# A planner's durations, and where third products stand, in a two-layer graph kernel on one core

## The chip, the core and the metric

The kernel runs on one core of one Trainium2 chip. The metric is the device time of one execution in microseconds (us), the median of several runs. Five engines work side by side and meet at semaphores: PE (TensorE, matrix products), DVE (VectorE), ACT (ScalarE), POOL (GpSimd) and SP (SyncE, which here only issues transfers).

## The reference, cut to what matters

`x` has the shape 64 x 256 x 512, `adj` is a 256 x 256 matrix of zeros and ones, about 3% of them ones. Two layers follow each other, each with a layer norm and a ReLU ahead of it and a residual around it.

```python
h = jnp.maximum(_layernorm(x, axis=-1), 0.0)
q, k, v = h @ Wq.T, h @ Wk.T, h @ Wv.T
rel = adj.T[None] * jnp.einsum('bnd,bmd->bnm', q, k)
rel = rel / jnp.linalg.norm(rel, axis=2, keepdims=True)
x = x + jnp.einsum('bnm,bmd->bnd', rel, v)
h = jnp.maximum(_layernorm(x, axis=-1), 0.0)
y = jnp.einsum('nm,bmd->bnd', adj, h)
x = x + jnp.einsum('bnd,do->bno', y, weight) + bias
```

## The kernel before, in words

**Work in pairs.** Two of the 64 batches are worked on at once, as a pair of 512 rows: 32 pairs. `Wq` and `Wk` are multiplied into one matrix m ahead of everything, so that scores are h m h'.

**Three products for one.** Every operand of a product with full precision is kept as three parts: u (the value rounded by a scaled copy on ACT), l (what is left) and s (a cross term of both). A bank of PSUM gets the u products, then the l products; ACT then scales the bank in place by a number close to one (line 361); then the third products, those of s, are added. So third products wait for a scaling, and the scaling waits for the l products. The parts are made by `split_right_ps` (ACT makes u at line 265, DVE s at line 266, DVE l from s at line 268) and by `split_left_ps` (ACT u at 274, DVE l at 275, DVE s at 276).

**Stages of a pair**, by operand names in the profile: `g_stage` (h with m, four banks, split into gy_u, gy_l, gy_s), `v_stage` (h with wv, four blocks, split into `v_low` and `late_parts`), `scores` (h with gy, two banks of 256-column products; then multiplied by adj into `h_rel`, squared and summed), `gather` of the pair before (adj with the second layer's h), `turn_scores` (scores turned and split into rel_u, rel_l and rel_s), `mix` of the pair before (gy, now holding y, with w), `attend` (rel with v, four banks). Scores are turned by 16 small transfers and DVE (lines 480 to 487) or, in pairs 0, 1 and 31, by PE (line 467).

**Who decides the order.** The kernel doesn't emit its instructions one after another. Stages call `plan.add(engine, cost, fn, reads, writes)`, and `Plan.order` (lines 58 to 102) then lays down one order for all engines. Costs and landing times are in microseconds. The matmul groups keep the order in which they were added. From their running sum each op gets a due time, going back over what depends on it. A list scheduler then runs through model time: on the engine that comes free first, it takes, of the ops that are ready at that moment, the one that is due first. It never keeps an engine idle for an op that becomes ready a little later. Between engines it counts `SYNC`, 0.12. On the chip every engine works through its own list in order.

**`unit`** (lines 349 to 367) is one bank. `first` yields the u and l products (three groups in `three`, lines 369 to 388: two of u, one of l; two groups in `attend`, u and l). Then `finish` runs what waits in the list `waiting`, which is the third products of the bank before and its drain. Then it adds the scaling and puts its own third products into `waiting`:

```python
        for cost, fn, reads in first(ps):
            plan.add("PE", cost, fn, reads, [key])
        finish(plan)
        ...
        plan.add("ACT", 0.49, lambda: A.activation(ps, ps, AF.Copy, scale=ONE), [], [key])
```

So the third products of one bank stand behind both the u and the l products of the next. Ahead of `scores` stands v block 1 (right operand wv_s). Ahead of `attend` stands the last bank of `mix` (w_s); in pair 31 it is v block 3, and in pair 0 nothing, as line 725 calls `finish` first.

Of the kernel before, what the change touches and what calls it, by code (L numbers as in the profile page):

```python
# [27 lines left out]
class Plan:  # L28


    SYNC = 0.12
# [26 lines left out]
    def order(self):  # L58
        ops = self.ops
        at, ideal = 0.0, {}  # L60
        for n, (engine, cost, *_) in enumerate(ops):
            if engine == "PE":
                ideal[n] = at
                at += cost
        due = [ideal.get(n, at + 50.0) for n in range(len(ops))]
        for n in range(len(ops) - 1, -1, -1):
            engine, cost, _, before, _, early = ops[n]
            due[n] -= early
            for m in before:
# [44 lines left out]
def kernel(  # L114
# [142 lines left out]
    MM, HALF = 0.231, 0.1185  # L257
# [3 lines left out]
    def split_right_ps(plan, ps, key, parts, names, at, cost=0.49):  # L261
# [4 lines left out]
        plan.add("DVE", 0.63, lambda: V.scalar_tensor_tensor(  # L266
            s(), f(u()), ONE, ps, op0=ALU.mult, op1=ALU.subtract), [*key, *ku], ks)
        plan.add("DVE", 0.6, lambda: V.scalar_tensor_tensor(  # L268
            l(), f(s()), -CROSS, f(u()), op0=ALU.mult, op1=ALU.add), [*ku, *ks], kl)

    def split_left_ps(plan, ps, key, parts, names, at):
        u, l, s = (p(at) for p in parts)
        ku, kl, ks = names
        plan.add("ACT", 0.49, lambda: A.activation(u, ps, AF.Copy, scale=NEAR), [key], ku)
        plan.add("DVE", 0.6, lambda: V.tensor_sub(l, ps, f(u)), [key, *ku], kl)  # L275
        plan.add("DVE", 0.6, lambda: V.scalar_tensor_tensor(
            s, f(l), CROSS + 1.0, ps, op0=ALU.mult, op1=ALU.subtract), [key, *kl], ks)
# [3 lines left out]
    def load(plan, i, src=None, name="fresh"):  # L281

        dst = fresh if name == "fresh" else ring[i % 2]
        plan.add("SP", 0.65, lambda: SP.dma_start(out=dst, in_=xs[i]), [], keys(name, TC), lands=5.5)

    def norm(plan, i, layer, src, name):

        st, mv, rs, nb = stats[layer][i % 2]
        k = f"n{layer}{i % 2}"
        for c in range(TC):  # L290
            def chunk(c=c):
                V.bn_stats(st[:, c, :], src[:, c, :])  # L292
                V.bn_aggr(mv[:, c, :], st[:, c, :])
            plan.add("DVE", 0.84, chunk, [(name, c)], [(k, c)])
        every = keys(k, TC)
        plan.add("DVE", 0.12, lambda: V.tensor_scalar(
            rs, mv[:, :, 1], 0.0, EPS, op0=ALU.max, op1=ALU.add), every, [(k, "rs")])
# [5 lines left out]
        plan.add("DVE", 0.25, end, every, [(k, "rs")])  # L303

        def relu(dst, c):
            A.activation(dst, src[:, c, :], AF.Relu, bias=nb[:, c : c + 1], scale=rs[:, c : c + 1])
        return relu, [(k, "rs")]

    def h_rows(plan, i, src=fresh, name="fresh"):
        relu, needs = norm(plan, i, 0, src, name)  # L310
        for c in range(TC):
            plan.add("ACT", 0.72, lambda c=c: relu(h_rel[:, c, :] if name == "x0" else h_cols[:, c], c),
                     [(name, c), *needs, *([("h_rel", 0)] if c else [])], [("h_rel", c)] if c else keys("h_rel", TC))
# [4 lines left out]
    def h_turn(plan):  # L318
        def turn(k):
            ht[k] = room(f"ht{k}", 2, T, tag=f"h_s{k}")  # L320
            for d in range(2):
                V.transpose(ht[k][:, d].rearrange("p (c k s) -> p c k s", c=TC, k=J), h_placed[:, :, 2 * k + d])  # L322
        for k in range(2):
            plan.add("DVE", 1.16, lambda k=k: turn(k), placed_all, [("h_s", 2 * k), ("h_s", 2 * k + 1)])
# [6 lines left out]
    def h_parts(plan):  # L331
        u, l = h
        for k in range(2):
# [5 lines left out]
            plan.add("DVE", 1.14, lambda k=k, at=at: V.tensor_sub(  # L339
                l[:, at], ht[k], f(u[:, at])), [*ks, *ku], kl)  # L340
            plan.add("DVE", 1.14, lambda k=k: h_third(k), [*ku, *kl], ks)
# [7 lines left out]
    def unit(plan, first, second, drain, on=None):  # L349
# [3 lines left out]
        if on is not None:  # L353
            plan.add("ACT", 0.58, lambda: A.copy(ps, on), ["bias"], [key])
        for cost, fn, reads in first(ps):
# [5 lines left out]
        plan.add("ACT", 0.49, lambda: A.activation(ps, ps, AF.Copy, scale=ONE), [], [key])  # L361
# [67 lines left out]
    def scores(plan, i):  # L429
        rn = norms[i % 2]  # L430
        for b in range(NB):
# [7 lines left out]
            def drain(ps, key, b=b):  # L439
# [4 lines left out]
                plan.add("DVE", 0.6, lambda: V.tensor_mul(  # L444
# [3 lines left out]
                for k in range(NC):  # L448
                    plan.add("ACT", 0.53, lambda k=k: A.activation(
                        columns(ps)[:, k], dst[:, k], AF.Square, accum_out=rn[:, b, k : k + 1]),  # L450
                        [("h_rel", b)], [key, (f"rn{i % 2}", b, k)])
            unit(plan, first, second, drain)

    def turn_scores(plan, i):
# [3 lines left out]
        plan.add("DVE", 0.12, lambda: V.reciprocal(rn, rn), [], sums)  # L458
        if by_pe(i):
            u, l = (part.rearrange("p b t k n -> p b (t k n)") for part in rel_p)  # L460
            for b in range(NB):
# [11 lines left out]
                plan.add("ACT", 0.49, lambda ps=ps, b=b: A.activation(  # L473
                    u[:, b], ps, AF.Copy, scale=NEAR), [key], [("rel_u", b)])
                plan.add("DVE", 0.63, lambda ps=ps, b=b: V.tensor_sub(  # L475
                    l[:, b], ps, f(u[:, b])), [key, ("rel_u", b)], [("rel_l", b)])
                plan.add("DVE", 0.6, third, [("rel_u", b), ("rel_l", b)],
# [4 lines left out]
        for b in range(NB):  # L482
            for k in range(NC):
                plan.add("DVE", 0.33, lambda b=b, k=k: V.transpose(
# [11 lines left out]
        plan.add("DVE", 1.14, lambda: V.tensor_sub(l, flat_raw(), f(u)), [*halves, *rel_u], rel_l)  # L496
        plan.add("DVE", 1.14, lambda: V.scalar_tensor_tensor(
            whole(rel_third()), f(l), CROSS, f(u), op0=ALU.mult, op1=ALU.subtract), [*rel_u, *rel_l], halves)

    def attend(plan, i, exact):  # L500
        slot, rn = i % 2, norms[i % 2]
        for c in range(TC):
# [16 lines left out]
            def drain(ps, key, b=b, n=n, c=c):  # L519
                plan.add("DVE", 0.63, lambda: V.scalar_tensor_tensor(  # L520
# [4 lines left out]
            unit(plan, first, second, drain)  # L525

    def layer_1(plan, i, exact):
        slot = i % 2
        relu, needs = norm(plan, i, 1, ring[slot], f"x{slot}")
        for c in range(TC):  # L530
            x_c = [(f"x{slot}", c), *needs]
            if not exact:
                plan.add("ACT", 0.72, lambda c=c: relu(changing("late", "h2", 8, D)[:, c], c), x_c,
# [4 lines left out]
            plan.add("ACT", 0.72, lambda c=c: relu(raw()[:, c % 2], c), x_c,  # L538
                     [("raw", 0), ("raw", 1)] if not c else k)
            plan.add("ACT", 0.53, lambda c=c, u=u: A.copy(late(u), raw()[:, c % 2]), k, [("late", u)])  # L540
            plan.add("DVE", 0.6, lambda c=c, u=u, l=l: V.tensor_sub(
# [29 lines left out]
    def mix(plan, i, blocks_of=range(4)):  # L571
        slot = i % 2
        for c in blocks_of:
# [5 lines left out]
            def drain(ps, key, c=c):  # L579
                plan.add("DVE", 0.6, lambda: V.tensor_add(  # L580
# [64 lines left out]
    adjt = []  # L645
# [4 lines left out]
    def first_turn(plan):  # L650

        u, l = h
        for d in range(DC):
# [6 lines left out]
            plan.add("ACT", 0.49, lambda ps=ps, d=d: A.activation(  # L660
                u[:, d], ps, AF.Copy, scale=NEAR), [key], [("h_u", d)])
            plan.add("DVE", 0.63, lambda ps=ps, d=d: V.tensor_sub(
                l[:, d], ps, f(u[:, d])), [key, ("h_u", d)], [("h_l", d)])
        for k in range(2):
            kept = [(f"h_{q}", d) for q in "ul" for d in (2 * k, 2 * k + 1)]
            plan.add("DVE", 1.14, lambda k=k: h_third(k), kept, [("h_s", 2 * k), ("h_s", 2 * k + 1)])
# [7 lines left out]
    def first_g(plan):  # L674

        banks = [next_bank() for _ in range(DC)]
        for k in range(3):
            for e, (ps, key) in enumerate(banks):
# [3 lines left out]
                if k == 2:  # L682
                    plan.add("ACT", 0.49, lambda ps=ps: A.activation(ps, ps, AF.Copy, scale=ONE), [], [key])
# [21 lines left out]
    def pairs(exact):  # L705
# [6 lines left out]
        plan.add("ACT", 0.49, lambda: A.copy(adjt[0].rearrange("p m n -> p (m n)"), bank[6]), [("bank", 6)], ["adjt"])  # L712
# [83 lines left out]
```

## Time and profile before

| | us |
|---|---|
| median of 3 runs | 1561.76 (1561.21 to 1562.63) |
| the profiled execution | 1560.76 |
| its span, first to last instruction | 1559.0 |

The profile is of one execution. Its span is 1.76 us shorter than the time of that same execution. In three stretches the engines were busy as follows (us; the answer to a question for stretches of the span):

| stretch | length | PE | DVE | ACT |
|---|---|---|---|---|
| 24.7 to 66 | 41.30 | 39.33 | 40.93 | 28.13 |
| 800 to 847.4 (one pair) | 47.40 | 47.40 | 41.82 | 31.89 |
| 1511 to 1530 | 19.00 | 18.24 | 17.43 | 12.31 |

"Busy" on PE is to be read with care, since a matmul's end is modelled and not measured. The distance from one matmul's start to the next is the better measure. "Late start" below means: later than the regular distance of that shape.

### The profile page before, as it was taken

Reading aid. Unit: us, or ns where it says so; the run is one execution under the profiler, and the core shown is the slowest. Engines: PE = TensorE matmul, PEld = TensorE weight load, DVE = VectorE, ACT = ScalarE, POOL = GpSimd, SP = SyncE. Lnnn points to the kernel's source line nnn. Section 1 sums busy time; section 2 is a strip of 40 time slices with the busy share of each in tenths; the row PEclk is TensorE's granted clock in tenths of the full one; section 3 lists DMA queues with packets and bytes.
Section 4 is the critical chain, followed back from the end, with each engine's and each line's share of the span. In section 5 each row is a group of like instructions: output and inputs, shape, how many; then the busy total and the mean of one; then the engine's idle time right before and its main releaser. Section 6 shows DMA issues by size and latency. Waiting matters only on the chain.

```text
span 1559.0 us, 22543 instructions
## 1 busy us (share of the span) xinstructions
PE 1548.2 (99%) x8046; PEld 1323.5 (85%) x8046; DVE 1355.3 (87%) x2419; ACT 1022.7 (66%) x1941; POOL 24.3 (2%) x39
## 2 busy tenths in 40 slices
PE   9999999999999999999999999999999999999998
PEld 6788888888888888888888888888888888888886
DVE  6997889898889988898988899888989888989786
ACT  5567666666667676666676675766666766666654
POOL 0000000000000000000000000000000000000000
PEclk9999999999999999999999999999999999999999
DMA  5321333223333223333233332233332233322211
GB/s 199 112 83 41 122 111 120 77 71 110 118 113 119 66 78 117 114 117 90 72 96 118 112 122 68 77 114 114 116 106 71 81 121 111 120 71 76 85 55 56
DMA packets 91112, 153.63 MB, mean 99 GB/s; under 512 B 17136, under 2 KB 32240, under 8 KB 90992
## 3 DMA queue, kind: packets, MB, share of 16 engines
q1 hardware_dynamic: 80768, 116.46, 24.7%
q0 software_dynamic: 8432, 32.51, 5.7%
q10 hardware_dynamic: 1792, 3.15, 0.6%
q8 instruction: 65, 1.06, 0.3%
q14 instruction: 55, 0.45, 0.1%
HBM read 70.78 MB, written 33.55 MB: 67 GB/s over the span
## 4 chain that ended last, share of the span: by engine, by line
PE 95%; DVE 3%; DMA 1%; ACT 0%; issue 0%; ACTq 0%; DVEq 0%
PE bank L255 95%; DMA bias_bc<-in_L_gnn_bias_dram 1%; DMA x_ring<-in_x_dram 1%; DVE late_parts L266 0%; DVE late_parts L268 0%; DVE rel_s_parts L470 0%; DVE st L292 0%; DVE rel_l L475 0%; DVE gy_l L275 0%; DVE m_l L268 0%; DVE gy_l L268 0%; DVE wv_l L268 0%; DVE ht L322 0%; DVE wv_s L266 0%; DVE m_s L266 0%
## 5 line engine op out<-in xcount | busy, mean ns | idle before, releaser
L361 ACT ACTIVATE bank<-bank 128x512 f32<-128x512 f32 x572 | 333.5, 583 | 307.8 <-PE bank L255 304.2
L255 PE MATMUL bank<-wv_s,hs 128*128 128x512 f32 x512 | 137.8, 391 | 0.0
L255 PE MATMUL bank<-wv_u,h_u 128*128 128x512 f32 x512 | 137.5, 390 | 0.0
L255 PE MATMUL bank<-wv_l,h_l 128*128 128x512 f32 x512 | 136.9, 389 | 0.0
L255 PE MATMUL bank<-w_u,gy_u 128*128 128x512 f32 x512 | 136.9, 389 | 0.0
L255 PE MATMUL bank<-w_l,gy_l 128*128 128x512 f32 x512 | 136.9, 389 | 0.0
L255 PE MATMUL bank<-h_l,m_l 128*128 128x512 f32 x512 | 136.6, 389 | 0.1
L255 PE MATMUL bank<-w_s,gy_s 128*128 128x512 f32 x512 | 136.7, 389 | 0.0
L255 PE MATMUL bank<-h_u,m_u 128*128 128x512 f32 x512 | 136.5, 389 | 0.0
L255 PE MATMUL bank<-hs,m_s 128*128 128x512 f32 x512 | 136.4, 389 | 0.0
L266 DVE SCALAR_TENSOR_TENSOR gy_s<-gy_u,bank 128x512 fp32r<-128x512 f32 x128 | 86.2, 675 | 43.0 <-ACT gy_u L265 43.0
L255 PEld LDWEIGHTS bank<-h_l,m_l 128*128 128x128 f32 x512 | 96.0, 188 | 20.4 <-DVE h_l L339 0.5
L255 PEld LDWEIGHTS bank<-wv_l,h_l 128*128 128x128 f32 x512 | 96.1, 188 | 20.2
L255 PEld LDWEIGHTS bank<-h_u,m_u 128*128 128x128 f32 x512 | 96.0, 188 | 20.2 <-ACT m_u L265 0.2
L255 PEld LDWEIGHTS bank<-w_l,gy_l 128*128 128x128 f32 x512 | 96.1, 188 | 20.0
L255 PEld LDWEIGHTS bank<-hs,m_s 128*128 128x128 f32 x512 | 96.1, 188 | 19.9
L255 PEld LDWEIGHTS bank<-w_u,gy_u 128*128 128x128 f32 x512 | 96.0, 188 | 20.0
L255 PEld LDWEIGHTS bank<-w_s,gy_s 128*128 128x128 f32 x512 | 96.0, 188 | 20.0 <-ACT bank L361 0.2
L255 PE MATMUL bank<-adjt_r,late_parts 128*128 128x256 f32 x896 | 112.6, 277 | 0.0
L255 PEld LDWEIGHTS bank<-wv_s,hs 128*128 128x128 f32 x512 | 93.8, 188 | 18.3 <-ACT bank L361 0.7
L255 PEld LDWEIGHTS bank<-wv_u,h_u 128*128 128x128 f32 x512 | 93.7, 188 | 17.7
L255 PEld LDWEIGHTS bank<-adjt_r,late_parts 128*128 128x128 f32 x896 | 107.3, 188 | 0.0
(110 smaller groups left out, 3072.3 us busy)
## 6 DMA issues: line engine op xcount, KB each, us to landing
fresh<-in_x_dram SPq DMA_DIRECT2D x31, 1024.0 KB, 5.7
blocks<-h_rel SPq DMA_DIRECT2D x496, 64.0 KB, 2.0
x_ring<-in_x_dram SPq DMA_DIRECT2D x31, 1024.0 KB, 8.0
out_dram<-x_ring POOLq DMA_DIRECT2D x31, 1024.0 KB, 5.4
h_rel<-h_rel SPq DMA_DIRECT2D x464, 32.0 KB, 1.8
blocks<-in_L_gnn_Wv_dram ACTq DMA_DIRECT2D x1, 1024.0 KB, 11.1
x_ring<-in_L_gnn_weight_dram SPq DMA_DIRECT2D x1, 1024.0 KB, 12.3
out_dram<-x_ring SPq DMA_DIRECT2D x4, 256.0 KB, 2.3
```

The lines of the kernel that those rows point to most:

```text
L255: nc.tensor.matmul(out, left, right, start=first, stop=True, skip_group_check=True)
L266: plan.add("DVE", 0.63, lambda: V.scalar_tensor_tensor(s(), f(u()), ONE, ps, op0=ALU.mult, op1=ALU.subtract), [*key, *ku], ks)
L361: plan.add("ACT", 0.49, lambda: A.activation(ps, ps, AF.Copy, scale=ONE), [], [key])
```

## The change

It does three things. First, nearly all costs in the plan get new numbers, and loads get longer landing times. Second, the scheduler counts 0.11 (`CHAIN`) from the end of a DVE op to a DVE op that depends on it, where it counted nothing. Third, `unit` takes an argument `behind`: the number of the group ahead of which `finish` is called. In the first bank of `scores` it is 2 and in the first bank of `attend` it is 1, so in both the third products of the bank before come behind the u products and ahead of the l products. Elsewhere it is 9, which no group reaches, and `finish` is called where it was.

The core of the diff:

```diff
-    SYNC = 0.12
+    SYNC, CHAIN = 0.12, 0.11
...
-                when[m] = max(when[m], t + cost + lands + (0.0 if same else self.SYNC))
+                when[m] = max(when[m], t + cost + lands + (self.CHAIN * (engine == "DVE") if same else self.SYNC))
...
-    MM, HALF = 0.231, 0.1185
+    MM, HALF = 0.229, 0.1165
...
-    def unit(plan, first, second, drain, on=None):
+    def unit(plan, first, second, drain, on=None, behind=9):
...
-        for cost, fn, reads in first(ps):
+        for n, (cost, fn, reads) in enumerate(first(ps)):
+            if n == behind:
+                finish(plan)
             plan.add("PE", cost, fn, reads, [key])
         finish(plan)
...
-            unit(plan, first, second, drain)
+            unit(plan, first, second, drain, behind=9 if b else 2)
...
-            unit(plan, first, second, drain)
+            unit(plan, first, second, drain, behind=9 if c else 1)
```

The costs, old and new (us in the plan):

| op, its line before | old | new |
|---|---|---|
| ACT u part or scaling, 265, 274, 361, 473 | 0.49 | 0.50 |
| ACT copy of the bias into a bank, 354 | 0.58 | 0.50 |
| ACT relu, 306 | 0.72 | 0.76 |
| ACT squares 449, copy of a part 540 | 0.53 | 0.56 |
| DVE s part 266, rel_l 475, attend's drain 520 | 0.63 | 0.61 |
| DVE other 512-column ops | 0.60 | 0.605 |
| DVE ops over 1024 columns, 329, 339, 496, 497 | 1.14 | 1.135 |
| DVE turn of h, 322 (two transposes) | 1.16 | 1.24 |
| DVE turn of scores, 484 | 0.33 | 0.331 |
| DVE statistics of one chunk, 292 and 293 | 0.84 | 0.82 |
| DVE small ops, 296 and 458 | 0.12 | 0.20 |
| DVE 301 and 302 together | 0.25 | 0.37 |
| landing of a load into `fresh` | 5.5 | 6.0 |
| landing of a load into `x_ring` | 5.5 | 8.0 |

More of the change, by code (lines that the diff above doesn't have):

```diff
@@ L255, in mm, with split_right_ps @@
         nc.tensor.matmul(out, left, right, start=first, stop=True, skip_group_check=True)
-    MM, HALF = 0.231, 0.1185
-    def split_right_ps(plan, ps, key, parts, names, at, cost=0.49):
+    MM, HALF = 0.229, 0.1165
+    def split_right_ps(plan, ps, key, parts, names, at, cost=0.5):
         key = key if isinstance(key, list) else [key]
@@ L265, in split_right_ps @@
         plan.add("ACT", cost, lambda: A.activation(u(), ps, AF.Copy, scale=NEAR), key, ku)
-        plan.add("DVE", 0.63, lambda: V.scalar_tensor_tensor(
+        plan.add("DVE", 0.61, lambda: V.scalar_tensor_tensor(
             s(), f(u()), ONE, ps, op0=ALU.mult, op1=ALU.subtract), [*key, *ku], ks)
-        plan.add("DVE", 0.6, lambda: V.scalar_tensor_tensor(
+        plan.add("DVE", 0.605, lambda: V.scalar_tensor_tensor(
             l(), f(s()), -CROSS, f(u()), op0=ALU.mult, op1=ALU.add), [*ku, *ks], kl)
@@ L273, in split_left_ps @@
         ku, kl, ks = names
-        plan.add("ACT", 0.49, lambda: A.activation(u, ps, AF.Copy, scale=NEAR), [key], ku)
-        plan.add("DVE", 0.6, lambda: V.tensor_sub(l, ps, f(u)), [key, *ku], kl)
-        plan.add("DVE", 0.6, lambda: V.scalar_tensor_tensor(
+        plan.add("ACT", 0.5, lambda: A.activation(u, ps, AF.Copy, scale=NEAR), [key], ku)
+        plan.add("DVE", 0.605, lambda: V.tensor_sub(l, ps, f(u)), [key, *ku], kl)
+        plan.add("DVE", 0.605, lambda: V.scalar_tensor_tensor(
             s, f(l), CROSS + 1.0, ps, op0=ALU.mult, op1=ALU.subtract), [key, *kl], ks)
@@ L283, in load @@
         dst = fresh if name == "fresh" else ring[i % 2]
-        plan.add("SP", 0.65, lambda: SP.dma_start(out=dst, in_=xs[i]), [], keys(name, TC), lands=5.5)
+        plan.add("SP", 0.65, lambda: SP.dma_start(out=dst, in_=xs[i]), [], keys(name, TC), lands=6.0 if name == "fresh" else 8.0)
     def norm(plan, i, layer, src, name):
@@ L293, in chunk @@
                 V.bn_aggr(mv[:, c, :], st[:, c, :])
-            plan.add("DVE", 0.84, chunk, [(name, c)], [(k, c)])
+            plan.add("DVE", 0.82, chunk, [(name, c)], [(k, c)])
         every = keys(k, TC)
-        plan.add("DVE", 0.12, lambda: V.tensor_scalar(
+        plan.add("DVE", 0.2, lambda: V.tensor_scalar(
             rs, mv[:, :, 1], 0.0, EPS, op0=ALU.max, op1=ALU.add), every, [(k, "rs")])
@@ L302, in end @@
             V.scalar_tensor_tensor(nb, mv[:, :, 0], -1.0, rs, op0=ALU.mult, op1=ALU.mult)
-        plan.add("DVE", 0.25, end, every, [(k, "rs")])
+        plan.add("DVE", 0.37, end, every, [(k, "rs")])
         def relu(dst, c):
@@ L311, in h_rows @@
         for c in range(TC):
-            plan.add("ACT", 0.72, lambda c=c: relu(h_rel[:, c, :] if name == "x0" else h_cols[:, c], c),
+            plan.add("ACT", 0.76, lambda c=c: relu(h_rel[:, c, :] if name == "x0" else h_cols[:, c], c),
                      [(name, c), *needs, *([("h_rel", 0)] if c else [])], [("h_rel", c)] if c else keys("h_rel", TC))
@@ L323, in h_turn @@
         for k in range(2):
-            plan.add("DVE", 1.16, lambda k=k: turn(k), placed_all, [("h_s", 2 * k), ("h_s", 2 * k + 1)])
+            plan.add("DVE", 1.24, lambda k=k: turn(k), placed_all, [("h_s", 2 * k), ("h_s", 2 * k + 1)])
     def h_third(k):
@@ L338, in h_parts @@
                 u[:, at], ht[k], AF.Copy, scale=NEAR), ks, ku)
-            plan.add("DVE", 1.14, lambda k=k, at=at: V.tensor_sub(
+            plan.add("DVE", 1.135, lambda k=k, at=at: V.tensor_sub(
                 l[:, at], ht[k], f(u[:, at])), [*ks, *ku], kl)
-            plan.add("DVE", 1.14, lambda k=k: h_third(k), [*ku, *kl], ks)
+            plan.add("DVE", 1.135, lambda k=k: h_third(k), [*ku, *kl], ks)
     waiting = []
@@ L347, in finish @@
             waiting.pop(0)()
-    def unit(plan, first, second, drain, on=None):
+    def unit(plan, first, second, drain, on=None, behind=9):
         ps, key = next_bank(on=on)
         if on is not None:
-            plan.add("ACT", 0.58, lambda: A.copy(ps, on), ["bias"], [key])
-        for cost, fn, reads in first(ps):
+            plan.add("ACT", 0.5, lambda: A.copy(ps, on), ["bias"], [key])
+        for n, (cost, fn, reads) in enumerate(first(ps)):
+            if n == behind:
+                finish(plan)
             plan.add("PE", cost, fn, reads, [key])
@@ L360, in unit @@
             return
-        plan.add("ACT", 0.49, lambda: A.activation(ps, ps, AF.Copy, scale=ONE), [], [key])
+        plan.add("ACT", 0.5, lambda: A.activation(ps, ps, AF.Copy, scale=ONE), [], [key])
         def rest():
@@ L443, in columns @@
                     return part.rearrange("p (k t j s) -> p k t j s", k=NC, t=NC, j=J)
-                plan.add("DVE", 0.6, lambda: V.tensor_mul(
+                plan.add("DVE", 0.605, lambda: V.tensor_mul(
                     *(part.rearrange("p k t j s -> p (k t) j s") for part in (
@@ L448, in drain @@
                 for k in range(NC):
-                    plan.add("ACT", 0.53, lambda k=k: A.activation(
+                    plan.add("ACT", 0.56, lambda k=k: A.activation(
                         columns(ps)[:, k], dst[:, k], AF.Square, accum_out=rn[:, b, k : k + 1]),
                         [("h_rel", b)], [key, (f"rn{i % 2}", b, k)])
-            unit(plan, first, second, drain)
+            unit(plan, first, second, drain, behind=9 if b else 2)
     def turn_scores(plan, i):
@@ L457, in turn_scores @@
         plan.add("ACT", 0.2, lambda: A.activation(rn, rn, AF.Sqrt), [], sums)
-        plan.add("DVE", 0.12, lambda: V.reciprocal(rn, rn), [], sums)
+        plan.add("DVE", 0.2, lambda: V.reciprocal(rn, rn), [], sums)
         if by_pe(i):
@@ L472, in turn_scores @@
                 plan.add("PE", 0.44, go, [("h_rel", b)], [key])
-                plan.add("ACT", 0.49, lambda ps=ps, b=b: A.activation(
+                plan.add("ACT", 0.5, lambda ps=ps, b=b: A.activation(
                     u[:, b], ps, AF.Copy, scale=NEAR), [key], [("rel_u", b)])
-                plan.add("DVE", 0.63, lambda ps=ps, b=b: V.tensor_sub(
+                plan.add("DVE", 0.61, lambda ps=ps, b=b: V.tensor_sub(
                     l[:, b], ps, f(u[:, b])), [key, ("rel_u", b)], [("rel_l", b)])
-                plan.add("DVE", 0.6, third, [("rel_u", b), ("rel_l", b)],
+                plan.add("DVE", 0.605, third, [("rel_u", b), ("rel_l", b)],
                          [("raw", 0), ("raw", 1)] if not b else [("raw", 1)])
@@ L483, in turn_scores @@
             for k in range(NC):
-                plan.add("DVE", 0.33, lambda b=b, k=k: V.transpose(
+                plan.add("DVE", 0.331, lambda b=b, k=k: V.transpose(
                     raw()[:, b].rearrange("p (t k j s) -> p t k j s", t=NC, k=NC, j=J)[:, :, k], placed[:, b, k]),
@@ L495, in turn_scores @@
         plan.add("ACT", 0.96, lambda: A.activation(u, flat_raw(), AF.Copy, scale=NEAR), halves, rel_u)
-        plan.add("DVE", 1.14, lambda: V.tensor_sub(l, flat_raw(), f(u)), [*halves, *rel_u], rel_l)
-        plan.add("DVE", 1.14, lambda: V.scalar_tensor_tensor(
+        plan.add("DVE", 1.135, lambda: V.tensor_sub(l, flat_raw(), f(u)), [*halves, *rel_u], rel_l)
+        plan.add("DVE", 1.135, lambda: V.scalar_tensor_tensor(
             whole(rel_third()), f(l), CROSS, f(u), op0=ALU.mult, op1=ALU.subtract), [*rel_u, *rel_l], halves)
@@ L519, in drain @@
             def drain(ps, key, b=b, n=n, c=c):
-                plan.add("DVE", 0.63, lambda: V.scalar_tensor_tensor(
+                plan.add("DVE", 0.61, lambda: V.scalar_tensor_tensor(
                     ring[slot][:, c, :], ps, rn[:, b, n : n + 1], ring[slot][:, c, :],
@@ L532, in layer_1 @@
             if not exact:
-                plan.add("ACT", 0.72, lambda c=c: relu(changing("late", "h2", 8, D)[:, c], c), x_c,
+                plan.add("ACT", 0.76, lambda c=c: relu(changing("late", "h2", 8, D)[:, c], c), x_c,
                          keys("late", 12)[4:] if not c else [("late", 4 + c)])
@@ L537, in layer_1 @@
             k = [("raw", c % 2)]
-            plan.add("ACT", 0.72, lambda c=c: relu(raw()[:, c % 2], c), x_c,
+            plan.add("ACT", 0.76, lambda c=c: relu(raw()[:, c % 2], c), x_c,
                      [("raw", 0), ("raw", 1)] if not c else k)
-            plan.add("ACT", 0.53, lambda c=c, u=u: A.copy(late(u), raw()[:, c % 2]), k, [("late", u)])
-            plan.add("DVE", 0.6, lambda c=c, u=u, l=l: V.tensor_sub(
+            plan.add("ACT", 0.56, lambda c=c, u=u: A.copy(late(u), raw()[:, c % 2]), k, [("late", u)])
+            plan.add("DVE", 0.605, lambda c=c, u=u, l=l: V.tensor_sub(
                 late(l), raw()[:, c % 2], f(late(u))), [*k, ("late", u)], [("late", l)])
@@ L579, in drain @@
             def drain(ps, key, c=c):
-                plan.add("DVE", 0.6, lambda: V.tensor_add(
+                plan.add("DVE", 0.605, lambda: V.tensor_add(
                     ring[slot][:, c, :], ps, ring[slot][:, c, :]), [key], [(f"x{slot}", c)])
@@ L659, in first_turn @@
             plan.add("PE", 0.44, go, keys("h_rel", TC), [key])
-            plan.add("ACT", 0.49, lambda ps=ps, d=d: A.activation(
+            plan.add("ACT", 0.5, lambda ps=ps, d=d: A.activation(
                 u[:, d], ps, AF.Copy, scale=NEAR), [key], [("h_u", d)])
-            plan.add("DVE", 0.63, lambda ps=ps, d=d: V.tensor_sub(
+            plan.add("DVE", 0.61, lambda ps=ps, d=d: V.tensor_sub(
                 l[:, d], ps, f(u[:, d])), [key, ("h_u", d)], [("h_l", d)])
@@ L665, in first_turn @@
             kept = [(f"h_{q}", d) for q in "ul" for d in (2 * k, 2 * k + 1)]
-            plan.add("DVE", 1.14, lambda k=k: h_third(k), kept, [("h_s", 2 * k), ("h_s", 2 * k + 1)])
+            plan.add("DVE", 1.135, lambda k=k: h_third(k), kept, [("h_s", 2 * k), ("h_s", 2 * k + 1)])
     def last_m(plan):
@@ L682, in first_g @@
                 if k == 2:
-                    plan.add("ACT", 0.49, lambda ps=ps: A.activation(ps, ps, AF.Copy, scale=ONE), [], [key])
+                    plan.add("ACT", 0.5, lambda ps=ps: A.activation(ps, ps, AF.Copy, scale=ONE), [], [key])
                 plan.add("PE", 4 * MM, go, [
@@ L711, in pairs @@
         adjt[:] = [turned_adj[:, P - 16 : P - 16 + NC * N].rearrange("p (c n) -> p c n", c=NC)]
-        plan.add("ACT", 0.49, lambda: A.copy(adjt[0].rearrange("p m n -> p (m n)"), bank[6]), [("bank", 6)], ["adjt"])
+        plan.add("ACT", 0.5, lambda: A.copy(adjt[0].rearrange("p m n -> p (m n)"), bank[6]), [("bank", 6)], ["adjt"])
         first_turn(plan)
```

## The prediction

> **What bounds the kernel now.** I read the page's busy table first, then the chain that ended last, then TensorE's waits, then the timeline where the two moved products stand.
>
> ```profile
> PE 1548.2 (99%) x8046; PEld 1323.5 (85%) x8046; DVE 1355.3 (87%) x2419; ACT 1022.7 (66%) x1941; POOL 24.3 (2%) x39
> ```
>
> PE is busy 99%. Matmul ends are modelled, so I don't take that as proof; the chain in order of time is better (start, length, what):
>
> ```profile
> 61.60 0.57 DVE rel_s_parts L470
> 62.17 2.28 DVE h_l L339 x2
> 64.50 25.06 PE bank L255 x148
> 89.56 1.09 PE bank L467 x8
> 90.66 1421.00 PE bank L255 x7416
> ...
> 1523.95 0.70 DVE late_parts L268
> 1524.70 28.45 PE bank L255 x139
> ```
>
> From 90.66 to 1511.7 us the chain is PE and nothing else. Before it stands DVE (from 24.7 to 64.5 us), after it some 13 us of DVE and ACT and then PE again. One pair has 168 matmuls of 512 columns, which start 0.2267 us apart (four in 0.907), and 80 of 256 columns, 0.118 apart: 38.1 + 9.4 = 47.5 us. The first product with rel_l recurs every 47.45 us (248.8, 296.3, ...). So a pair lasts just its matmuls: the middle has nothing to give, only something to lose. All that PE waits for visibly is:
>
> ```profile
> PE bank L255 <- DVE rel_s_parts L470: 1.2, 1, 1.2
> PE bank L255 <- DMA wk_sb<-in_L_gnn_Wk_dram: 1.1, 1, 1.1
> PE bank L255 <- POOL h_rel L612: 1.0, 1, 1.0
> PE bank L255 <- DVE late_parts L268: 0.7, 1, 0.7
> PE bank L255 <- DVE rel_l L475: 0.6, 1, 0.6
> ```
>
> The two with DMA and POOL lie ahead of the plan. Counted as late starts against the regular step, 54 to 65 us lose 3.3 us and 1515 to 1525 lose 1.4: at most 4.7 us, 0.3%, is there to gain.
>
> **What the Trainium skill says.** "TensorE: Matmul & The Clock Gate", section "Wait — 56ns, not 53.3ns?", gives 215.7 ns from start to start of warm 512-column matmuls; here it is 226.7, and the trace's step is my floor. "ScalarE: Activation LUTs", section "What ACT_TABLE_LOAD costs", gives 186 ns + 0.833 N for an ACTIVATE with immediates, 612 ns at N = 512; line 361 shows 583. "VectorE: DVE Perf Modes", section "The DRAIN you can't avoid", says that a semaphore between chained ops costs nothing extra; the trace differs: four independent L266 begin 0.60 us apart, but L268, which reads what L266 wrote, begins 0.71 later (43.46 to 44.17). That is the 0.11 of CHAIN. "Perfetto Trace Analysis", section "Tensor Engine Instruction (MATMUL, LD_WEIGHTS)", says that ACT and DVE are strict FIFO: an order in the plan is an order on the chip, and an op put ahead of an urgent one is paid in full.
>
> **The change part by part.** No instruction is added or removed; matmuls, scalings, splits and DMAs are the same in number. Two things move.
>
> *Third products, scores.* In the timeline (start, length, engine, line, op):
>
> ```profile
> 839.82 1.11 PE L255 MATMUL bank<-h_u,gy_u 128*128 128x256 f32 x8
> 840.76 1.11 PE L255 MATMUL bank<-h_l,gy_l 128*128 128x256 f32 x8
> 841.71 1.09 PE L255 MATMUL bank<-wv_s,hs 128*128 128x512 f32 x4
> ```
>
> The four wv_s products of v block 1 go between the other two rows, in all 32 pairs. The gy_l products start 0.91 us later, so gy_l has 0.91 more; its last L268 ends at 840.40, 0.36 ahead of its first reader (the steady median over pairs is 0.47). The third products start 0.95 us earlier, so block 1's bank must be scaled (L361) earlier. That scaling runs from 839.15 to 839.74; the new start is 840.76. 1.02 us remain: cost 0.
>
> *Third products, attend.* PE, then ACT, at one pair:
>
> ```profile
> 818.06 0.62 PE L255 MATMUL bank<-v_low,rel_u 128*128 128x512 f32 x2
> 818.52 0.39 PE L255 MATMUL bank<-v_low,rel_l 128*128 128x512 f32 x1
> ...
> 818.97 1.07 PE L255 MATMUL bank<-w_s,gy_s 128*128 128x512 f32 x4
> ```
>
> ```profile
> 817.49 0.58 ACT L361 ACTIVATE bank<-bank 128x512 f32<-128x512 f32 x1
> 818.01 1.50 ACT L306 ACTIVATE h_rel<-fresh,nb,rs 128x512 f32<-128x512 f32 x2
> 819.41 0.58 ACT L361 ACTIVATE bank<-bank 128x512 f32<-128x512 f32 x1
> ```
>
> w_s moves from 818.97 to 818.52, and rel_l from 818.52 to 819.43, in 31 pairs: in pair 0 `finish` runs ahead of attend and nothing waits. rel_l ends 0.90 us ahead of its reader (steady median) and gets 1.81. The mix bank's scaling ends at 818.07; 0.45 remain. The tight one is attend's own first bank. Its last rel_l product starts at 819.65; L361 follows a last start by 0.42 (820.56 to 820.98), so 820.07; it takes 0.58, PE follows by 0.05 (57.65 to 57.70 in pair 0): 820.70. The bank's own third product still starts at 820.78, since only w_s and rel_l trade places. Between them there were 1.81 us of other products, now 0.91: 0.08 us remain. ACT must be free at 820.07, and it is: the relus (L306) hand over at 819.41, and the scaling that stands there moves away. Cost 0, while ACT keeps that order; if a relu (0.71 us a step) stands there, up to 0.71 - 0.08 = 0.63 us per pair.
>
> *The plan's costs.* This reorders ACT, DVE and SP; which ops swap, the trace can't show, so I bound it. With CHAIN, the second of two chained DVE ops isn't ready when the first ends, so the scheduler takes any other ready op first. That pushes the chained op back by the inserted op, at most one turn (1.24 us), and saves 0.11 of idle time. Covers after the moves: gy_l 0.36 + 0.91 = 1.27, rel_l 1.81, rel_s 1.91, the y parts 1.97 ahead of w_l. All hold 1.24 once: 0 in the middle. Without that cover: 0.1 us per pair is 3.1 us. DVE's saved idle is worth nothing there, since it is no bound (41.8 of 47.4 us busy). The longer landing times of loads move SP's issues, the 16 placements of 0.65 us queued behind them too; h_l has 4.86 us ahead of its reader, which I take as cover.
>
> *The front*, 24.7 to 66 us, is where DVE is the chain (40.93 us busy of 41.30), so order counts. Saved chain idle: some 3 to 5 steps of 0.11, up to 0.5. Swaps: a w_l (0.60) that leaves the way, or a turn (1.24) that gets into it. Bounds: -2.8 (the 0.73, 0.30, 1.34, 0.26 of late starts and some small ones) to +1.5. I take -0.5, the idle alone.
>
> *The end.* In the last pair v block 3's wv_s moves 0.45 us forward. Now its chain is L265 at 1522.60, L266 at 1523.23, L268 at 1523.95, PE at 1524.70. DVE is held by block 2's L268 until 1522.69, so the new chain is 1522.7, 1523.4, PE at 1524.1: -0.6. Bounds -1.3 (all of it) and +0.5 (a bias copy, 0.59, stands ahead of L265).
>
> Sum: 0 + 0 + 0 - 0.5 - 0.6 = -1.1 us of the span of 1559.0, so 1557.9. The profiled execution took 1560.76, 1.76 around the span: 1559.7. The median of the runs shown is 1.0 higher, 1561.76, so 1560.7.
>
> **The rivals.**
> 1. *A scaling becomes the wait, in each pair.* Place: attend's first bank (cover 0.08) or the mix bank ahead of it (0.45). Mechanism: relus cost 0.76 in the plan and turns 1.24, so the plan sees ACT free at another moment and starts a relu just ahead of the scaling. Price: half of 0.63, 0.3 us, times 30: +9, so about 1570.5. It decides from a scaling that starts after 820.15 in that pair. For it: pair 0 has this very order already, with its scaling behind a relu (57.04 in place of 56.89), and PE loses 0.09 there. Against: ACT has only four relus there, and they end 0.66 us early. Chance 0.27.
> 2. *The better model clears the front.* DVE no longer takes weight splits ahead of rel and late parts, and the end closes: -3.6, 1558.1. For it: 4.8 us of w splits ran on DVE ahead of 54.8. Against: most ran when nothing urgent was ready. 0.13.
> 3. *A long op slips into the front's chain*, a turn ahead of a rel third: +1.2 there, -0.6 at the end: 1562.4. 0.14.
> 4. *My forecast*, which includes that the new durations, mostly within 3% of the old, change almost no order: 1560.7. 0.46.
>
> **How the numbers follow.** A measurement here tells about 0.2%, 3.1 us, from no change. Faster by that needs 1558.6 or less: rival 2 nearly whole and a little of mine, 0.12 + 0.02 = 0.14. Slower: rival 1 but for its cheap end, 0.24, and 0.02 of rival 3: 0.26. Within: 0.60. My own case has 1559 to 1562.5. The range takes in rival 2's time and rival 1 up to its middle, leaving out some 0.18: 1558.0 to 1570.5.
>
> **What would show it.** Right: the period stays 47.4 to 47.5 us; wv_s and w_s stand between u and l; PE's late starts at 54 to 65 and at 1523 to 1525 shrink. Wrong: PE waits for ACT L361 some 30 times at rel_s_parts or w_s (rival 1), or for gy_l or rel_l (a cover I took too wide), or the period grows by 0.1 us or more.

## The result, and the profile after

The changed kernel took 1573.6 us (median of 6 runs, 1572.63 to 1574.02), the kernel before, run beside it, 1561.57. The ratio is 1.0075, with a 95% interval of 1.0064 to 1.0085: 12 us slower. The profiled execution's span grew from 1559.0 to 1570.8 us. The forecast was 1560.7, the range ended at 1570.5.

The page's busy table hardly tells it:

```profile
PE 1555.9 (99%) x8046; PEld 1319.9 (84%) x8046; DVE 1332.8 (85%) x2419; ACT 1023.9 (65%) x1941; POOL 24.3 (2%) x39
```

The count of instructions is the same, and PE still looks 99% busy, because a matmul that starts late is drawn longer (below, the first rel_l product 0.50 us in place of 0.39). PE's waits after (who waited, for whom: us in total, times, longest) name the place, but too little of the amount:

```profile
PE bank L255 <- DVE rel_s_parts L500: 3.0, 16, 0.5
...
PE bank L255 <- DVE rel_l L499: 0.5, 1, 0.5
```

So I count late starts: the distance from one matmul's start to the next beyond the regular step of its shape (226.5, 116 and 109 ns for 512, 256 and 128 columns), where it is over 12 ns. Summed in us over four stretches of the span, for all kernels of this study (each ratio is to runs of before beside it, whose median lay between 1561.38 and 1561.91; the late starts are those of the one profiled execution, which for some kernels was up to 1.5 us above the median):

| kernel | median | ratio to before, 95% | to 24.7 us | 24.7 to 100 | 100 to 1505 | from 1505 |
|---|---|---|---|---|---|---|
| before | 1561.57 | | 12.0 | 4.1 | 0.4 | 1.4 |
| changed | 1573.60 | 1.0064 to 1.0085 | 12.0 | 2.7 | 14.2 | 0.5 |
| chain0 | 1563.78 | 1.0007 to 1.0020 | 11.5 | 8.8 | 1.4 | 0.8 |
| chain_only | 1571.39 | 1.0046 to 1.0077 | 12.1 | 3.6 | 11.0 | 1.6 |
| wait_chain | 1562.54 | 0.9998 to 1.0014 | 12.1 | 4.9 | 1.2 | 0.6 |
| behind_off | 1580.26 | 1.0104 to 1.0135 | 11.7 | 3.8 | 19.6 | 1.6 |
| behind_only | 1562.68 | 0.9998 to 1.0015 | 10.6 | 5.7 | 2.4 | 1.3 |
| rel_direct | 1559.50 | 0.9977 to 0.9990 | 12.4 | 2.7 | 1.2 | 0.5 |
| lands_old | 1573.13 | 1.0056 to 1.0088 | 11.2 | 4.6 | 13.7 | 0.5 |
| costs_only | 1562.24 | 0.9993 to 1.0010 | 10.5 | 7.0 | 2.3 | 1.3 |
| direct_last | 1564.49 | 1.0011 to 1.0025 | 11.6 | 3.9 | 5.2 | 0.5 |
| direct_turns | 1566.24 | 1.0018 to 1.0041 | 12.3 | 2.7 | 7.1 | 0.5 |
| chain_behind | 1562.61 | 0.9998 to 1.0015 | 11.8 | 3.7 | 3.5 | 0.5 |
| direct_rs | 1571.60 | 1.0049 to 1.0083 | 12.2 | 3.2 | 11.8 | 0.5 |

The changed kernel gains 1.4 us at the front and 0.9 at the end, and loses 13.8 in the middle. The loss lies in attend alone. Of the 29 pairs whose scores DVE turns, 14 (nearly every second one) lose 0.81 us, one of them 1.16; most of the others lose 0.08. One of the 14, PE by the timeline (start, length, engine, line, op; in brackets the idle time before it):

```profile
583.71 1.07 PE L255 MATMUL bank<-w_s,gy_s 128*128 128x512 f32 x4
584.91 0.50 PE L255 MATMUL bank<-v_low,rel_l 128*128 128x512 f32 x1
585.25 0.39 PE L255 MATMUL bank<-late_parts,rel_l 128*128 128x512 f32 x1
...
586.18 0.40 PE L255 MATMUL bank<-late_parts,rel_l 128*128 128x512 f32 x1
586.74 0.47 PE L255 MATMUL bank<-v_low,rel_s_parts 128*128 128x512 f32 x1 [0.16 <-DVE rel_s_parts L500]
587.05 0.39 PE L255 MATMUL bank<-late_parts,rel_s_parts 128*128 128x512 f32 x1
```

Four products of 512 columns take 0.91 us, so rel_l should have started at 584.62: it is 0.29 late, the next product 0.11, the first rel_s product 0.33, the next 0.08. Together 0.81 us. The third products do stand where the change puts them: w_s between rel_u and rel_l.

The chain that ended last shows for this stretch (start, length, what) who was late:

```profile
579.55 0.35 DVE rel_s_raw L487
579.90 0.58 DVE x_ring L583
580.48 1.00 DVE rel_s_raw L487 x3
581.48 2.24 DVE h_l L339 x2
583.73 1.14 DVE rel_l L499
584.86 0.60 DVE x_ring L583
585.46 1.14 DVE rel_s_parts L500
586.60 0.14 issue
586.74 73.26 PE bank L255 x383
```

It has no ACT scaling in it. Line 487 turns the scores, four times; ACT makes rel_u from them; DVE makes rel_l (499) and then rel_s (500). Among these stand ops that nobody waits for yet: a residual add (x_ring) after the first turn, two subtractions for h_l, another residual add between rel_l and rel_s. Before, the same stage ran on DVE like this (a timeline):

```profile
813.39 1.38 DVE L484 STREAM_TRANSPOSE rel_s_raw<-h_rel 128x256 f32<-128x256 f32 x4
814.70 0.65 DVE L580 TENSOR_TENSOR x_ring<-bank,x_ring 128x512 f32<-128x512 f32 x1
815.27 1.20 DVE L339 TENSOR_TENSOR h_l<-ht,h_u 128x1024 fp32r<-128x1024 f32 x1
816.40 1.21 DVE L496 TENSOR_TENSOR rel_l<-rel_s_raw,rel_u 128x1024 fp32r<-128x1024 f32 x1
817.64 1.23 DVE L497 SCALAR_TENSOR_TENSOR rel_s_parts<-rel_l,rel_u 128x1024 fp32r<-128x1024 f32 x1
818.79 1.22 DVE L339 TENSOR_TENSOR h_l<-ht,h_u 128x1024 fp32r<-128x1024 f32 x1
```

Four turns in one go, one h_l ahead of rel_l, rel_s right behind it. In the pairs of the changed kernel that don't wait, a late part stands between the turns, and one h_l, not two, ahead of rel_l:

```profile
627.00 0.40 DVE L487 STREAM_TRANSPOSE rel_s_raw<-h_rel 128x256 f32<-128x256 f32 x1
627.33 0.65 DVE L268 SCALAR_TENSOR_TENSOR late_parts<-late_parts 128x512 fp32r<-128x512 f32 x1
627.90 1.09 DVE L487 STREAM_TRANSPOSE rel_s_raw<-h_rel 128x256 f32<-128x256 f32 x3
...
629.49 1.20 DVE L339 TENSOR_TENSOR h_l<-ht,h_u 128x1024 fp32r<-128x1024 f32 x1
630.61 1.21 DVE L499 TENSOR_TENSOR rel_l<-rel_s_raw,rel_u 128x1024 fp32r<-128x1024 f32 x1
631.74 1.22 DVE L339 TENSOR_TENSOR h_l<-ht,h_u 128x1024 fp32r<-128x1024 f32 x1
632.88 1.22 DVE L500 SCALAR_TENSOR_TENSOR rel_s_parts<-rel_l,rel_u 128x1024 fp32r<-128x1024 f32 x1
```

The second h_l gets ahead by a hair. In the waiting pair ACT makes rel_u here:

```profile
581.51 1.06 ACT L498 ACTIVATE rel_u<-rel_s_raw 128x1024 fp32r<-128x1024 f32 x1 [0.95 <-DVE rel_s_raw L487]
```

It ends at 582.57, and DVE came free of its first h_l at 582.52. The order was not decided on the chip, though, but in the plan, and by the plan's numbers it is just as close. rel_l is ready 0.12 + 0.96 + 0.12 = 1.20 us after the last turn (to ACT, rel_u's cost, back to DVE) if ACT is free. An h_l that follows the last turn directly ends after 1.135, so rel_l isn't ready and the second h_l is. With the residual add behind the turns, as before, DVE comes free of its first h_l only after 0.605 + 1.135 = 1.74, and rel_l is next. So the residual add that slipped in among the turns costs nothing by itself, since it only changed its place; it lets a whole h_l in ahead of rel_l.

### The profile page after: what moved, and what is told of

Its sections match the earlier page's. It is cut to its first block, busy times and chain, and to the rows that moved or that the text cites. A ratio compares the mean times of both kernels' runs of the same rounds, so it can differ in the third digit from the quotient of the medians.

```text
span 1570.8 us, 22584 instructions
## 1 busy us (share of the span) xinstructions
PE 1555.9 (99%) x8046; PEld 1319.9 (84%) x8046; DVE 1332.8 (85%) x2419; ACT 1023.9 (65%) x1941; POOL 24.3 (2%) x39
## 4 chain that ended last, share of the span: by engine, by line
PE 73%; DVE 14%; SPq 7%; DMA 3%; issue 1%; ACT 1%; DVEq 0%; ACTq 0%
PE bank L255 73%; SPq L231 7%; DVE h_l L339 2%; DVE ht L322 2%; DMA h_rel<-h_rel 2%; DVE rel_s_raw L487 1%; DVE x_ring L583 1%; DVE rel_s_parts L500 1%; DVE rel_l L499 1%; DVE late_parts L268 1%; DVE h_rel L447 1%; DVE late_parts L266 1%; DVE gy_l L275 1%; DMA bias_bc<-in_L_gnn_bias_dram 1%; DMA x_ring<-in_x_dram 1%
## 5 line engine op out<-in xcount | busy, mean ns | idle before, releaser
L447 DVE TENSOR_TENSOR h_rel<-bank,adjt_r 128x512 f32<-128x512 f32 x64 | 44.1, 690 | 85.2 <-PE bank L255 76.7
## 6 DMA issues: line engine op xcount, KB each, us to landing
x_ring<-in_L_gnn_weight_dram SPq DMA_DIRECT2D x1, 1024.0 KB, 12.4
```

The lines of the kernel that those rows point to most:

```text
L447: plan.add("DVE", 0.605, lambda: V.tensor_mul(*(part.rearrange("p k t j s -> p (k t) j s") for part in (dst, columns(ps), columns(f(adjt[0 ...
```

## The experiments

Theory A: CHAIN lets the scheduler put other DVE ops between the chained ops that lead to rel_l and rel_s. Theory B, rival 1 of the prediction: a bank's scaling is the wait, since the third products moved. Theory C: SP. The loads got longer landing times, and SP's own waits changed much. Before it waited for a store twice, 20.6 us in all; in the changed kernel the line is

```profile
SPq L284 <- DMA out_dram<-x_ring: 575.2, 30, 31.5
```

That is, the load of the next residual stands at the head of SP's queue, 19 us a pair, with the placements of h, and then the next load into `fresh`, behind it.

### One part away, one part alone

**chain0**, the changed kernel without the 0.11:

```diff
-    SYNC, CHAIN = 0.12, 0.11
+    SYNC, CHAIN = 0.12, 0.0
```

> The changed kernel with CHAIN set to 0.0, all else as changed. Theory A (the 0.11 makes the scheduler put other DVE ops between the chained ops that lead to rel_l and rel_s, so PE waits for them in attend): the waits of 16 to 30 pairs at rel_l and rel_s vanish, period 47.4 to 47.5 us, total 1558 to 1562 us. Theory B (the moved third products leave too little time for a bank's scaling): no change, 1572 to 1575. Theory C (the longer landing times put the x_ring load at the head of SP's queue and delay the placements): no change, 1572 to 1575.

1563.78 us. The middle falls from 14.2 to 1.4 us of late starts; A holds there, and B falls. C falls as it was put, since the long landing times are still in. But SP's waits for the store went back as well (19.4 us, twice), so this run alone doesn't part DVE's order from SP's. The total missed its band by 2 us at the front, 8.8 against 2.7 (in an execution 1.4 us above the median): the new costs without the 0.11 order the front worse, so CHAIN is also what gains there.

**chain_only**, the kernel before with the 0.11 alone:

```diff
-    SYNC = 0.12
+    SYNC, CHAIN = 0.12, 0.11
...
-                when[m] = max(when[m], t + cost + lands + (0.0 if same else self.SYNC))
+                when[m] = max(when[m], t + cost + lands + (self.CHAIN * (engine == "DVE") if same else self.SYNC))
```

> The kernel before with the 0.11 alone; old costs, old landing times, third products at their old place. Theory A: all 29 middle pairs get two h_l subtractions ahead of rel_l and a residual add between rel_l and rel_s, and rel_l is wanted 0.9 us earlier than in the changed kernel, so each loses 0.8 to 1.3 us: 1583 to 1600 us. Theories B and C: as before, 1560 to 1563.

1571.39 us. As expected, 29 pairs get the bad order and 29 wait for rel_l; B and C, which expected no change, fall; SP waits for the store only twice here, 50.8 us in all. But each pair loses 0.37 us in the mean, not 0.8 to 1.3. The reason is in the table further down: with the old costs the turns start 1 us earlier against PE.

**behind_off**, the changed kernel with `behind=9` in both calls:

```diff
-            unit(plan, first, second, drain, behind=9 if b else 2)
+            unit(plan, first, second, drain, behind=9)
...
-            unit(plan, first, second, drain, behind=9 if c else 1)
+            unit(plan, first, second, drain, behind=9)
```

> The changed kernel with the third products at their old place in both stages. Theory A: rel_l is wanted 0.9 us earlier, while the order on DVE stays, so half of the pairs lose 1.2 to 1.4 us in place of 0.8: 1577 to 1585 us. Theory B: the wait goes, 1559 to 1563. Theory C: as the changed kernel or slower, 1573 to 1580.

1580.26 us, where A had it. Far from costing something, the moved third products save 6.7 us of what CHAIN loses. B is out as the cause.

**behind_only**, the kernel before with that part alone (`behind` as in the change).

> The kernel before with the third products moved alone; old costs, no CHAIN. Theory A: DVE's order in the middle is the old one, so no pair waits: 1560 to 1562 us (the end 0.5 us better). Theory B: 8 to 15 us slower than before, 1569 to 1577. Theory C: as before.

1562.68 us, not to be told from before (0.9998 to 1.0015), and not B's 1569. It is 0.7 us above A's band. All 30 pairs start the second rel_s product 0.04 us late, 1.2 us in all, which before they don't.

**lands_old**, the changed kernel with the old landing times:

```diff
-lands=6.0 if name == "fresh" else 8.0)
+lands=5.5)
```

> The changed kernel with the old landing time of 5.5 us for all loads. Theory A: the same DVE order, 29 pairs of which half wait: 1571 to 1576 us. Theory C: the placements move forward again and the wait goes, 1559 to 1563. Theory B: 1572 to 1575.

1573.13 us, the same loss (13.7 in the middle). SP still waits 571 us there, so the run alone doesn't free the placements; that SP's wait alone costs nothing is shown by rel_direct below.

**costs_only**, the kernel before with the new costs alone.

> The kernel before with the new costs alone; no CHAIN, old landing times, third products at their old place. Theory A: no pair waits in the middle, 1558 to 1563 us. If the new costs alone put DVE's order at risk: over 1566.

1562.24 us, no change (0.9993 to 1.0010). New costs alone are harmless in the middle.

**chain_behind**, the kernel before with CHAIN and the moved third products, old costs.

> The kernel before with CHAIN and the moved third products, old costs and landing times. If CHAIN makes rel_l 0.37 us late against its old place, as in chain_only, the move alone covers it: the rel_l wait goes and what is left is at rel_s, 0 to 0.1 us a pair, 1560 to 1565 us. Then the new costs are needed for the changed kernel's loss. If CHAIN with the move suffices for that loss: 1570 to 1578.

1562.61 us, no change (0.9998 to 1.0015). All 29 pairs still have the bad order, but the 0.37 us of chain_only are covered by the move. So the changed kernel's loss needs two things at once: the insertions that CHAIN allows, and the new costs. What the new costs add is shown further down.

### Which insertions

**rel_direct**, the changed kernel, but CHAIN isn't counted ahead of the four turns of scores and ahead of rel_s; every other chained op keeps it:

```diff
+        self.direct = set()
...
-(self.CHAIN * (engine == "DVE") if same else self.SYNC))
+(self.CHAIN * (engine == "DVE" and m not in self.direct) if same else self.SYNC))
...
+                plan.direct.add(len(plan.ops) - 1)
```

The last line stands behind each turn's `plan.add` and behind that of rel_s. So what is left out is the 0.11 counted into these ops; the expectations say "after" for it.

> The changed kernel, but CHAIN isn't counted after the four turns of scores and after rel_s, that is into the ops from the turns on; all other chained ops keep it. Theory A in its narrow form (the loss is on the way turns, rel_u, rel_l, rel_s): nearly all of it vanishes, 1557 to 1562 us. If the loss is from insertions elsewhere (late parts, gy): 1568 to 1575. Theories B and C: 1572 to 1575.

1559.50 us: the loss is gone (1.2 in the middle), the gains at both ends stay (2.7 and 0.5), and it is faster than before, 0.9977 to 0.9990. DVE runs the stage in the old order again:

```profile
576.16 1.41 DVE L488 STREAM_TRANSPOSE rel_s_raw<-h_rel 128x256 f32<-128x256 f32 x4
577.50 0.65 DVE L586 TENSOR_TENSOR x_ring<-bank,x_ring 128x512 f32<-128x512 f32 x1
578.08 1.21 DVE L340 TENSOR_TENSOR h_l<-ht,h_u 128x1024 fp32r<-128x1024 f32 x1
579.20 1.22 DVE L501 TENSOR_TENSOR rel_l<-rel_s_raw,rel_u 128x1024 fp32r<-128x1024 f32 x1
580.45 1.23 DVE L502 SCALAR_TENSOR_TENSOR rel_s_parts<-rel_l,rel_u 128x1024 fp32r<-128x1024 f32 x1
```

And SP waits as in the changed kernel, so C is out as the whole cause; SP's wait alone costs nothing here:

```profile
SPq L285 <- DMA out_dram<-x_ring: 577.0, 30, 31.5
```

**direct_turns** leaves CHAIN out ahead of the turns alone.

> The changed kernel, with CHAIN left out after the four turns of scores alone; rel_l to rel_s keeps it. If the residual add between the turns is what lets the second h_l subtraction pass ahead of rel_l, all pairs get the order of the better half, with an h_l subtraction between rel_l and rel_s, and late starts in the middle come to 1 to 3 us: 1559 to 1562 us. If the op between rel_l and rel_s counts by itself: 1564 to 1572.

1566.24 us. All 28 pairs have one h_l ahead of rel_l, and no rel_l is late, as expected. But what stands between rel_l and rel_s counts by itself, which I had put second. It is a whole h_l:

```profile
580.76 1.21 DVE L501 TENSOR_TENSOR rel_l<-rel_s_raw,rel_u 128x1024 fp32r<-128x1024 f32 x1
581.89 1.22 DVE L340 TENSOR_TENSOR h_l<-ht,h_u 128x1024 fp32r<-128x1024 f32 x1
583.03 1.22 DVE L502 SCALAR_TENSOR_TENSOR rel_s_parts<-rel_l,rel_u 128x1024 fp32r<-128x1024 f32 x1
```

rel_s ends at 584.25 and PE's product starts at 584.39, 0.15 late, with 0.08 behind it: 7 us over the pairs.

**direct_rs** leaves it out ahead of rel_s alone.

> The changed kernel, with CHAIN left out ahead of the rel_s op alone, so rel_s follows rel_l at once; the turns keep it, and a residual add stands between them in 28 pairs, with two h_l subtractions ahead of rel_l. In the waiting half of the changed kernel's pairs rel_l came 0.29 us late on this way (0.40 with what follows), and rel_s 0.33 on top. If the two insertions count one by one, rel_l's lateness stays, now in all 28 pairs, and rel_s's goes: 0.2 to 0.5 us a pair, 1565 to 1574 us. If the pair of rel_l and rel_s alone set the loss: 1559 to 1562.

1571.60 us. 27 pairs lose 0.31 and 0.11 us at rel_l, hardly anything at rel_s. So both insertions count, each by itself.

**wait_chain** keeps the 0.11 everywhere, but lets the scheduler wait for it:

```diff
-n = min((n for n in ready[engine] if when[n] <= t + 0.01), key=lambda n: (due[n], n))
+n = min((n for n in ready[engine] if when[n] <= t + (0.12 if engine == "DVE" else 0.01)), key=lambda n: (due[n], n))
```

> The changed kernel, but the scheduler also takes a DVE op that becomes ready within 0.12 us, if it is due first, so a chained op can follow at once. Theory A: the middle's waits vanish and the gain at the front and the end stays: 1557 to 1561 us. Theories B and C: 1572 to 1575.

1562.54 us, no change (0.9998 to 1.0014). In the middle A holds: 1.2 us, in all 29 pairs the old order. The gain at the front didn't stay (4.9 against 2.7), which I had not expected: there it is the filling of the 0.11 that helps.

**direct_last** is rel_direct with attend's third products moved in the last pair alone:

```diff
-            unit(plan, first, second, drain, behind=9 if c else 1)
+            unit(plan, first, second, drain, behind=9 if c or i + 1 < NP else 1)
```

> As rel_direct, and the third products in attend are moved in the last pair alone; those in scores are moved in all pairs. If the 0.04 us that each pair loses at the first rel_s product in rel_direct is the bank's scaling, whose cover the move cut to under 0.1 us, it goes: middle under 0.5 us of late starts in place of 1.2, total 1558 to 1559 us. If it is rel_s itself or something else, it stays: 1559.3 to 1560.5.

1564.49 us, 5 us slower than rel_direct, against expectation. The 0.04 at rel_s did go in every pair, so it is the scaling (rel_s itself ended 1.0 us before it was wanted in rel_direct). But rel_l, wanted 0.91 us earlier, now comes late by 0.06 to 0.07 and 0.11, in nearly all pairs.

### How the times add up

Starts on DVE against the first rel_u product of attend in the same pair (us, medians over the pairs; in the changed kernel over the waiting ones):

| | first turn of h | first turn of scores | rel_l | rel_s |
|---|---|---|---|---|
| before | -8.41 | -4.67 | -1.66 | -0.42 |
| chain_only | -8.41 | -4.83 | -0.66 | 1.07 |
| chain_behind | -8.41 | -4.83 | -0.66 | 1.07 |
| changed | -7.37 | -3.79 | 0.38 | 2.12 |
| changed, pair 30 alone | -8.41 | -4.83 | -0.66 | 1.07 |
| direct_rs | -7.38 | -3.79 | 0.38 | 1.63 |
| direct_turns | -7.38 | -3.79 | -0.75 | 1.51 |
| rel_direct | -7.37 | -3.79 | -0.75 | 0.49 |

An op of 1024 columns takes 1.22 us to its end. With the third products moved, PE wants rel_l at 1.36 and rel_s at 2.72; at their old place rel_l at 0.45. The changed kernel's rel_l ends at 0.38 + 1.22 = 1.60, late by 0.24; its rel_s at 3.34. rel_direct's end at 0.47 and 1.71. In chain_only rel_l ends at 0.56 with 0.45 wanted. Each row's waits follow from this, with 0.05 to 0.14 us from DVE's end to PE's start. In the waiting pairs it is 4.17 us from the first turn of scores to rel_l in place of 3.01, and 5.91 to rel_s in place of 4.25. And the turns themselves begin 0.88 us later than before.

That later start is in the seven kernels with the new costs and a CHAIN that is not waited for (changed, behind_off, lands_old, rel_direct, direct_turns, direct_rs, direct_last), and in none of the others. What stands ahead of the turn of h is seen on DVE, before and in the changed kernel:

```profile
808.71 0.69 DVE L268 SCALAR_TENSOR_TENSOR late_parts<-late_parts 128x512 fp32r<-128x512 f32 x1
809.65 1.30 DVE L322 STREAM_TRANSPOSE ht<-blocks 128x512 f32<-128x512 f32 x2 [0.25 <-DMA h_rel<-h_rel]
```

```profile
574.18 0.69 DVE L268 SCALAR_TENSOR_TENSOR late_parts<-late_parts 128x512 fp32r<-128x512 f32 x1
574.79 0.69 DVE L292 BATCH_NORM_STATS2 st<-fresh 128x6 f32<-128x512 f32 x1
575.51 0.18 DVE L293 BATCH_NORM_AGGREGATE mv<-st 128x2 f32<-128x6 f32 x1
575.89 1.30 DVE L322 STREAM_TRANSPOSE ht<-blocks 128x512 f32<-128x512 f32 x2 [0.19 <-DMA h_rel<-h_rel]
```

A chunk of the layer norm's statistics, of the rows loaded into `fresh`, has come ahead of it: 0.90 us. In the seven kernels two or three such chunks stand in the 8 us ahead of the turn of h, in all pairs from 3 to 29; in the others there is none. They stand there together with another order on SP. Before, SP issued in one pair (and, second, in the changed kernel):

```profile
771.64 12.98 SPq L231 DMA_DIRECT2D blocks<-h_rel  x16
784.66 0.58 SPq L284 DMA_DIRECT2D fresh<-in_x_dram  x1
785.36 0.47 SPq L284 DMA_DIRECT2D x_ring<-in_x_dram  x1
```

```profile
547.44 0.37 SPq L284 DMA_DIRECT2D x_ring<-in_x_dram  x1
550.96 10.01 SPq L231 DMA_DIRECT2D blocks<-h_rel  x16
561.07 0.53 SPq L284 DMA_DIRECT2D fresh<-in_x_dram  x1
```

With the x_ring load, which waits for the store, and the placements in front of it, the load into `fresh` lands about 16 us ahead of the first rel_u product, in place of 28.5. The four chunks of statistics that began 28 to 22 us ahead of that product before can't begin there any more. So theory C has a part after all: in the seven kernels SP waits 571 to 577 us for the store, in the others 19 to 51. It isn't the landing times, as lands_old has it too. This part is read from the traces; no run takes SP's order back alone.

The two halves can be told apart, all with the third products moved (late starts in the middle): neither, behind_only, 2.4 us; the insertions alone, chain_behind, 3.5; the later start alone, rel_direct, 1.2; both, changed, 14.2, and that in every second pair. Pair 30 of the changed kernel is the same trial in one pair: it has the bad order, but no further load, so no statistics stand ahead of its turns; rel_l isn't late, and it loses 0.04 us where pair 29 loses 0.81.

## Why the prediction was wrong

**What bounds the kernel** was right. The middle had nothing to give; a pair's matmuls stayed 47.5 us, and all the loss is the period's growth, to 47.95 us in the mean.

**Third products, scores** and **attend**, cost 0: right but for 0.04 us a pair. The cover of attend's first scaling was taken as 0.08 us, and there it failed by 0.04 (direct_last against rel_direct). The worth of the move was not counted at all: 6.7 us, once rel_l comes late.

**The plan's costs** is the step that failed. It said: "That pushes the chained op back by the inserted op, at most one turn (1.24 us)" and "All hold 1.24 once: 0 in the middle." That other ops would pass a chained one was right, and so was the price of one. What the covers were held against was too small, for two reasons. The way from the turns to rel_s has several chained ops (the four turns are chained as well, since all write `raw`), and each may be passed: rel_l came 1.16 us later after the first turn (one h_l), rel_s 1.66 (a residual add more). These alone the covers of 1.81 and 1.91 hold, as chain_behind shows. But the whole way also began 0.88 us later, and this was put at nothing: of SP's new order the step asked only about the placements ("h_l has 4.86 us ahead of its reader, which I take as cover"), not about the load into `fresh` and the statistics on DVE that follow it. So rel_l's 1.81 met 0.88 + 1.16 = 2.04, and rel_s's 1.91 met 0.88 + 1.66 = 2.54.

**The front**, -0.5: the late starts fell by 1.4, inside the bounds, but not by saved idle alone. The first rel_l product's lateness fell from 0.73 to 0.10 us. Small ops that before ran ahead of rel_l (lines 301, 302 and 458, at 52.04, 52.24 and 54.13) stand at 65.45 us and later in the changed kernel. **The end**, -0.6: by 0.9, inside the bounds. But the moved third products, the forecast's reason, leave 1.3 us there when they come alone (behind_only, 1.4 before); with CHAIN it is 0.5 (chain_behind). So both signs were right, in part by luck. Their sum of 2.3 us was covered by the middle's 13.8.

**Rival 1** had the right form: a small wait in about every pair, +9 us. Its mechanism was the wrong one: it was to be ACT's scaling behind a relu, and it was DVE's rel_l and rel_s behind h_l and residual adds. The sign that the prediction named for "a cover I took too wide", PE waiting for rel_l, is what the trace shows. **Rival 2** came half true in its size: with the loss removed, rel_direct keeps what the front and the end gained, 2.4 us faster than before, but the front still has 2.7 us of late starts. Its mechanism did not come: four w_l ops still run right ahead of rel_l (51.33 to 53.82 us in the changed kernel). **Rival 4's** words that the durations change almost no order were wrong for the change as a whole.

What stays open: which of the new costs, together with CHAIN, puts the x_ring load ahead on SP, and why it is every second pair that takes the bad order on DVE. No run takes single costs back.

## What to carry to other kernels

A truer duration can make a list scheduler's order worse, when the scheduler never waits: a latency of 0.11 us between two chained ops opens a door through which an op of 1.2 us may pass. When slack is compared with such insertions, follow the whole chain to the reader and allow one at every link, writes to the same buffer included. Then ask whether the chain still begins when it did: a load that another queue issues later moves the ops that read it, and here these came to stand ahead of the chain. Then either take the latency out for the one chain that feeds the bound engine, as rel_direct does, or let the scheduler wait; here the first kept the gain elsewhere and the second didn't.

## What the runs showed of the hardware

In these traces a wait cost PE more than its own length. After a late first product the next one starts late too, in the changed kernel by 0.11 us behind rel_l (584.91 to 585.25, a step of 0.34 in place of 0.23): 1.5 us in 14 pairs. It is the same 0.11 us behind waits of 0.08 us in the mean (direct_last), 0.31 (direct_rs) and 1.04 (behind_off). At rel_s the second product is 0.08 late in nearly all pairs, also where the first was on time; there the recorded start of the first seems to hide a short wait, which no run shows directly. And SP stood 19 us a pair in front of a load that waits for a store, 577 us in all, in the fastest of these kernels; what went with it was the later landing of the load behind it, and with that the later turns of scores.
